# Four-layer graph block on one core: scores of the first four samples computed apart, wv fetched last, weights fetched through three queues, TensorE fed with ones at the start

## The chip, the cores and the metric

One core of a Trainium2 chip. The metric is the device time of one execution in microseconds (us). Five engines work side by side, each through its own instructions in order: TensorE (PE; its weight loads are listed as PEld), VectorE (DVE), ScalarE (ACT), GpSimd (POOL) and SyncE (SP), which only issues transfers here. Work that depends on another engine waits on a semaphore.

## The reference, cut to what matters

Four layers, each `x = layernorm(x + f(x, adj))`, on 128 samples of 128 nodes with 512 features, all in float32. The change touches layer 0 alone:

```
Xw = X @ Wv + bv
sj = Xw @ aw[:d, 0];  si = Xw @ aw[d:, 0]
e = leaky_relu(sj[:, None, :] + si[:, :, None] + ab[0], 0.2)
transition = row-normalised(A * exp(e))
H = 0;  Xk = X
for k in range(3):                # Wk has shape (3, 512, 512)
    H = H + Xk @ Wk[k] + bk[k]
    Xk = transition @ Xk
x = layernorm(x + relu(H))
```

The kernel computes `H` as `Y0 + T (Y1 + T Y2)` with `Yk = X @ Wk[k]`, and the scores `si`, `sj` as `X @ (Wv @ aw)`, so that Wv enters only through two columns of 512 numbers.

## The kernel before

**Products by seven.** Layer 0 takes four samples at a time (two pairs; 32 such groups). The product of four samples with a weight matrix is done by Strassen's scheme (Winograd's form) on two levels: `twice` (line 846) goes through seven combinations of the samples (`lefts`, line 809, made by GpSimd) and of the weights, called B11, B21, T2, T1, B22, T3 and N4 in the order of their use, and for each `strassen` makes seven products, each with a 128x128 block on the left and a row of weights on the right. That is 49 products a group. The right side is 386 columns wide (`QW`): 128 for each of the three Wk, and two that give the scores. Each product is two MATMUL records in the trace (and two LDWEIGHTS). The seven weight combinations lie in seven tiles "first" (`w7`), and each holds its own seven combinations again.

**Making the weights.** `prepare0` (line 898) does it. Wv (1 MB) is fetched by SP in two halves, wk by ACT and SP: columns 0 to 255 of each matrix as "low" and "high" rows (12 transfers of 64 KB each, together 1.5 MB), then columns 256 to 511 (12 of 128 KB, 1.5 MB, on SP). VectorE forms Wv @ aw by eight dot products ("junk" rows) against aw, which TensorE has spread over the partitions; ScalarE copies the two columns into the weight tiles B11 and B21, beside the copies of wk. `combine` (line 514) then makes the inner combinations of B11, B21 and B22 on VectorE, with ScalarE holding operands in PSUM, `combine_apart` (line 509) those of B12 on GpSimd, and `combine_once_more` (line 520) the outer ones: T1 and T2 on VectorE in seven steps, then T3 and N4 on GpSimd in four long subtractions.

**After the 49 products.** The results of a sample pair are collected in an "out" tile (`R`), to which VectorE and ScalarE add or copy each bank of PSUM. There are three such tiles and a group needs two. From the score columns of `R`, which are complete when B11 and B21 are through, the transition matrix is made: two transposes on TensorE, ScalarE's Prelu and Exp, a multiplication with adj and the row sums on VectorE, a scaling on GpSimd, a trip through DRAM ("e") and a 32x32 transposition. Only then can the "t" products (`T` times the collected columns, 512 wide) run, and after the last of them the `R` tile is free for the next group but one.

**What sets the order.** The program first writes all operations down with a key (a wished place, about one unit per sample pair) and then `Plan.order` (line 239) plays the whole kernel through with estimated durations: each engine takes, of the operations that could begin next, the one with the smallest key (or the earliest due time in later rounds, except on TensorE, which always goes by key). What comes out is a fixed order for each engine. SP may fetch a thing that depends on nothing only when TensorE has reached its key in the play:

```
285            for k, t in ready[e].items():
286                if e == SP and ops[k][8] > reached and not ops[k][4]:
287                    continue
288                t = max(t, free[e], port[e] if ops[k][6] else 0)
289                if e == SP:
290                    t = max(t, *(landed[j - LANES] - ISSUE * j for j in range(len(ops[k][1]))))
```

Keys that matter: x of group 0 has -9.5, of group 1 -1.0, of group 2 1.0; the products of group 0 run from 0 in steps of .28 (T1 has .84), its scores have .8, its "t" products 2.0; group 1 has two more on each.

Of the kernel before, what the change touches and what calls it, by code (L numbers as in the profile page):

```python
# [14 lines left out]
OP = mybir.AluOpType  # L15
AX = mybir.AxisListType

P = 128
# [8 lines left out]
U = 2  # L27
# [15 lines left out]
WHENV, WHENS, WHENP, WHENO = (.9, 1.9), (2.2, 3.2), (3, 4), (3.5, 4.5)  # L43
LAG1, LAG2 = 1, 1.5
COMBINE = (-9, -2), (-.5, -.2), .1
SOFT = .2
PARKED, LATE = .95, 4
RAMP = 0, 0, .05, 4
# [75 lines left out]
def estimate(engine, name, out, args, kw):  # L124

    n = out.idx.size if isinstance(out, View) else 0
    views = [a for a in args if isinstance(a, View)]
    psum = any(a.tile.kind in PSUM for a in views)
    scalars = sum(isinstance(a, View) and a.idx.size == 1 for k, a in [*enumerate(args), *kw.items()] if k != "accum_out")
    if engine == PE:  # L130
        return 107 if name == "transpose" else (1.74 if n <= P else 1.68) * n
    if name == "dma_start":
        return ISSUE
    if engine == DVE:
        if name == "bn_aggr":
# [12 lines left out]
    return 60 if name == "memset" else (740 - 160 * scalars if scalars else 180 + 3.2 * n) if n > 8 else 215  # L148


def shares_port(engine, name, args, kw):

    if engine == POOL:
        return name != "memset"
    views = [a for a in args if isinstance(a, View)]
    sbuf = [a for a in views[1:] if a.tile.kind not in PSUM and a.idx.size > 1]
    if engine != DVE or not sbuf:
        return False
    if name in ("tensor_scalar", "tensor_copy"):
        return "accum_out" not in kw and views[0].idx.size > 1  # L160
    return len(sbuf) > 1
# [12 lines left out]
class Plan:  # L174
# [64 lines left out]
    def order(self, urgent=None):  # L239
# [41 lines left out]
        def look(e):  # L281

            can = []
            soonest = math.inf
            for k, t in ready[e].items():
                if e == SP and ops[k][8] > reached and not ops[k][4]:
                    continue
                t = max(t, free[e], port[e] if ops[k][6] else 0)
                if e == SP:
                    t = max(t, *(landed[j - LANES] - ISSUE * j for j in range(len(ops[k][1]))))  # L290
                new = {}
                for tile in ops[k][5]:
# [21 lines left out]
        while count < n:  # L314
# [15 lines left out]
            free[e] = end = t + o[2]  # L330
            if o[7]:
                end = pipe = max(pipe, t + BEGIN) + o[7]
                landed += [end + LANDED] * len(o[1])
                landed = landed[-LANES:]
            if e == PE and o[8] > reached:
                reached = o[8]
                stale.add(SP)
# [52 lines left out]
def kernel(  # L390
# [73 lines left out]
    def four():  # L464

        return tile_of("four", U, D)
# [35 lines left out]

    def held_in_bank(kind, block):

        p = tile_of(kind, QW)
        ac.copy(p, block)
        return p

# [11 lines left out]
    def combine_once_more(W):  # L520

        base = plan.key
        for n, i in enumerate((B11, T1, T2, B21, T3, B22, N4)):
            plan.key = base + .1 * n
            c12, c22 = (held_in_bank(k, W[j][:, i, 0]) for k, j in (("t0", B12), ("t1", B22)))
            for to, a, b in ((T1, c12, B11), (T2, c22, T1)):
                ve.tensor_tensor(W[to][:, i, 0], a, W[b][:, i, 0], OP.subtract)
        flat = [w.rearrange("p j o f -> p (j o f)") for w in W]
        for to, a, b in ((T3, T2, B11), (N4, B21, T2)):
            for at in (slice(0, 4 * QW), slice(4 * QW, 7 * QW)):  # L530
                po.tensor_tensor(flat[to][:, at], flat[a][:, at], flat[b][:, at], OP.subtract)

    def prep():

# [363 lines left out]
    def prepare0():  # L898
        h = D // 2
        plan.key = -9.7  # L900
        awr = four().rearrange("p u f -> p (u f)")
        sp.dma_start(awr[:1], aw.rearrange("f o -> o f"), run=2 * D, parts=1)
        W = WT["0"] = [tile_of("w7", 7, 1, QW, place=(B11, B21, T2, T1, B22, T3, N4).index(k)) for k in range(7)]
        stage = [W[T2 + m].rearrange("p j o f -> p (j o f)")[:, :C * D].rearrange("p (c f) -> p c f", f=D)
                 for m in range(3)]

        def fetch(queue, dst, src, chunks, columns, run):
            with plan.together():
# [6 lines left out]
            at = chunks, slice(half * h, half * h + h)  # L915
            fetch(queue, stage[m][:, at[0], at[1]], wk0[m], *at, h)

        low, high, every = slice(0, 2), slice(2, 4), slice(0, 4)
        st = [four() for _ in range(2)]
        for g, chunks in enumerate((low, high)):  # L920
            plan.key = -9.7 + .2 * g
            fetch(sp, st[g], wv0, chunks, slice(0, D), D)
        plan.key = -9
        for m in range(3):
            fetch_part(ac, m, low, 0)
        awc, bvc = fixed(2 * C, name="aw_c"), fixed(C, name="bv_c")
        ab_b, bk0b = fixed(1, name="ab_b"), row()
        with plan.together():
            for c, v, n in ((awc, aw, 2 * C), (bvc, bv0, C)):
                ac.dma_start(c, bass.AP(tensor=v.tensor, offset=v.offset, ap=[[1, P], [P, n]]), run=1)  # L930
            ac.dma_start(bk0b[:3], bk0, parts=3)
            ac.dma_start(ab_b, rows(ab, 1), run=1)
        for m in range(3):
            fetch_part(sp if m else ac, m, high, 0)
        ones = fixed(P, name="ones")
        po.memset(ones, 1.0)
        awb = [bank() for _ in range(2)]
        for k in range(2):
            pe.matmul(awb[k], ones[:1], awr[:1, k * D:(k + 1) * D], start=True, stop=True)
        two = fixed(C, 2, name="cols0")  # L940
        for c in range(C):
            for k in range(2):
                dot(two[:, c, k:k + 1], st[c // 2][:, c % 2], awb[k])
        plan.key = WHEN0[0] + .05
        for m in range(3):
            fetch_part(sp, m, every, 1)
        plan.key = -9
        for g, half, j in ((0, 0, B11), (1, 0, B21), (0, 1, B12), (1, 1, B22)):
            for m in range(3):
                ac.copy(W[j][:, :4, :, m * P:(m + 1) * P].rearrange("p (n c) o i -> p c n (o i)", n=2),  # L950
                        stage[m].rearrange("p c (n i) -> p c n i", i=P)[:, 2 * g:2 * g + 2, 2 * half:2 * half + 2])
            scores = W[j][:, :4, 0, 3 * P:]
            if half:
                po.memset(scores, 0.0)
            else:
                po.memset(scores[:, 2:], 0.0)
                ac.copy(scores[:, :2], two[:, 2 * g:2 * g + 2])
            plan.key = COMBINE[half][g]
            (combine_apart if j in (B12,) else combine)(W[j])
            plan.key = -9  # L960
        plan.key = COMBINE[2]
        combine_once_more(W)
        plan.key = -9
        p = bank()
        aws = fixed(C, name="aw_sum")
        ve.tensor_add(aws, awc[:, :C], awc[:, C:])
# [3 lines left out]
                          start=j == 0, stop=j == C - 1)  # L970
        ve.tensor_tensor(c0, p[:, :1], ab_b, OP.add)

        p = bank()
        pe.matmul(p, ones[:3], bk0b[:3], start=True, stop=True)
        p = p.rearrange("p (h n i) -> p h n i", h=2, n=2)
        ac.copy(bias[:, 0], p[:, 0])
        ve.tensor_tensor(bias[:, 1], p[:, 1], bias[:, 0], OP.subtract)
        plan.key = WHENT[0][0] - .1
        for kind in ("t0", "t1"):
            p = tile_of(kind, D)  # L980
            pe.matmul(p, ones[:3], bk0b[:3], start=True, stop=True)
# [8 lines left out]
    def layer0(i0):  # L990
# [16 lines left out]
        def fresh(bs):  # L1007
            def takes(d):
# [7 lines left out]
                                         "p5": put(d22, bs[:, 1]), "c21": put(d21, bs[:, 0])}  # L1016
            return takes

        twice(left, WT["0"], QW, lambda r, half: [R[r][:, b, 2 * half + n] for b in range(U) for n in range(2)],
              lambda r, half: [R[r][:, b, 2 * half:2 * half + 2] for b in range(U)],  # L1020
              [fresh(bias[:, half]) for half in range(2)], .28)
        yield
        loads = []
        for r, i in enumerate(both):
            A = load_adj(i)
            plan.key = base + WHENT[0][r]
            s = col(U)
            ac.activation(s, R[r][:, :, 0, 3 * P + 1], AF.Identity, bias=c0)
            pt = spread_pair([R[r][:, b, 0, 3 * P:3 * P + 1].to_broadcast([P, P]) for b in range(U)])
# [570 lines left out]
```

## Time and profile before

| | |
|---|---|
| time before, median of 3 runs | 5380.56 us (5377.26 to 5382.14) |
| the profiled execution's own time | 5377.98 us |
| its span in the trace | 5376.2 us |
| PE, share of the span | 99% (5307.6 us) |
| DVE, POOL, ACT | 82%, 73%, 45% |
| mean granted clock of TensorE | 0.998 |

A time outside the span (1.8 us) is what lies before the first and after the last instruction. Nearly all lines of the page are named L381, the line from which the planner emits; so an instruction is told by what it writes and reads: "bank<-first,four" is a product of layer 0 (weights "first", samples "four"), "first" as target is work on the weights, "out" the collecting of results, "junk" the dot products with Wv. A timeline line has the start, the time from the first start to the last end of the merged instructions, the engine, the operation and its count, and in brackets the idle time before and who ended it. The windows view has for each stretch its length, and per engine the busy time and the number of instructions; then the granted clock, the share of the DMA engines and GB/s.

### The profile page before, as it was taken

To read this page: it belongs to the slowest core of one execution; us is meant where nothing else is said; L and a number is where in the kernel's file an instruction comes from. 1 tells how busy PE (TensorE), PEld (TensorE's weight loads), DVE (VectorE), ACT (ScalarE), POOL (GpSimd) and SP (SyncE) were. 2 spreads that over 40 slices of the span, in tenths; PEclk is the share of its full clock that TensorE was granted. 3 is DMA by queue.
4 is the path that set the end of the run, shared out by engine and by line. 5 is a ranking of instruction groups with operands and counts; after the bars stand their busy time and mean duration, and the time that the engine had idled before them with its cause. 6 is when DMAs were issued, how large, how long until landed. Compare 5 with 4: busy or idle time off the path is not lost.

```text
span 5376.2 us, 92973 instructions
## 1 busy us (share of the span) xinstructions
PE 5307.6 (99%) x29039; PEld 4230.2 (79%) x29039; DVE 4423.1 (82%) x11721; ACT 2407.2 (45%) x6085; POOL 3906.2 (73%) x4937
## 2 busy tenths in 40 slices
PE   8999999999999999999999999999999999999998
PEld 4555555555888888888888889988998899889987
DVE  7788887887888888888888778887877888888876
ACT  3343343344544444444444344444444444444444
POOL 6777787676766666666666577777877777777776
PEclk9999999999999999999999999999999999999999
DMA  4544544445544454444444745555555455555543
GB/s 108 142 136 131 148 135 139 121 115 190 167 143 147 157 163 144 147 159 161 143 148 152 233 140 163 160 159 151 164 161 158 154 163 158 161 152 162 161 146 111
DMA packets 831143, 813.61 MB, mean 151 GB/s; under 512 B 258348, under 2 KB 631604, under 8 KB 830648
## 3 DMA queue, kind: packets, MB, share of 16 engines
q1 hardware_dynamic: 827650, 806.60, 48.9%
q8 instruction: 231, 3.78, 0.3%
q14 instruction: 264, 2.16, 0.1%
q10 hardware_dynamic: 2998, 1.06, 0.1%
HBM read 458.38 MB, written 349.04 MB: 150 GB/s over the span
## 4 chain that ended last, share of the span: by engine, by line
PE 88%; DVE 7%; issue 2%; DMA 1%; ACT 1%; POOL 1%; SPq 0%; ACTq 0%; DVEq 0%; POOLq 0%
PE bank L381 67%; PE t L381 21%; DVE four L381 2%; DVE out L381 1%; DVE col L381 1%; DVE first L381 1%; DVE junk L381 1%; POOL out L381 0%; ACT out L381 0%; DVE side L381 0%; ACT four L381 0%; DVE rows L381 0%; DVE bank L381 0%; DMA first<-in_L_gnn_Wk_dram 0%; SPq L381 0%
## 5 line engine op out<-in xcount | busy, mean ns | idle before, releaser
L381 PE MATMUL bank<-first,four 128*128 128x386 f32 (+3 forms) x6352 | 1748.6, 423 | 23.6 <-ACT first L381 9.9
L381 PEld LDWEIGHTS bank<-first,four 128*128 128x128 f32 (+2 forms) x6352 | 1089.3, 187 | 600.2 <-DVE out L381 101.9
L381 DVE TENSOR_TENSOR out<-bank,out 128x386 f32<-128x386 f32 (+1 forms) x1942 | 948.5, 507 | 253.1 <-PE bank L381 194.8
L381 DVE TENSOR_TENSOR four<-bank,four 128x256 f32<-128x256 f32 x1113 | 453.9, 416 | 151.3 <-PE bank L381 138.9
L381 POOL TENSOR_TENSOR out<-out 128x772 f32<-128x772 f32 (+3 forms) x249 | 341.6, 1381 | 272.9 <-DVE out L381 215.4
L381 POOL TENSOR_TENSOR four<-four 128x256 f32<-128x256 f32 (+2 forms) x434 | 351.5, 823 | 189.1 <-DVE four L381 140.6
L381 PE MATMUL bank<-first,out 128*128 128x256 f32 (+1 forms) x1746 | 432.4, 377 | 3.7 <-DVE four L381 1.6
L381 POOL TENSOR_TENSOR four<-four,four 128x256 f32<-128x256 f32 (+2 forms) x467 | 397.0, 855 | 10.0 <-PE bank L381 1.5
L381 POOL TENSOR_TENSOR col<-col,neghalf 128x2 f32<-128x2 f32 x320 | 227.9, 712 | 231.7 <-DVE col L381 230.5
L381 ACT COPY out<-bank 128x258 f32<-128x258 f32 (+2 forms) x489 | 194.9, 404 | 440.7 <-PE bank L381 359.9
L381 PEld LDWEIGHTS bank<-first,out 128*128 128x128 f32 (+1 forms) x1746 | 318.5, 188 | 65.4 <-issue 9.0
L381 ACT ACTIVATE four<-four,col,col 128x512 f32<-128x512 f32 (+1 forms) x355 | 308.5, 892 | 125.4 <-POOL col L381 118.9
L381 DVE TENSOR_TENSOR first<-bank,first 128x256 f32<-128x256 f32 (+1 forms) x591 | 240.4, 415 | 97.9 <-PE bank L381 89.3
L381 PE MATMUL bank<-first 128*128 128x128 f32 (+1 forms) x2132 | 297.6, 278 | 1.6 <-DVE four L381 1.6
L381 DVE BATCH_NORM_STATS2 col<-four 128x6 f32<-128x512 f32 x424 | 282.9, 681 | 10.5 <-ACT four L381 9.1
L381 ACT COPY four<-bank 128x256 f32<-128x256 f32 (+1 forms) x358 | 150.6, 424 | 303.8 <-PE bank L381 287.7
L381 PEld LDWEIGHTS bank<-first 128*128 128x128 f32 (+1 forms) x2132 | 270.0, 190 | 15.9 <-issue 4.0
L381 PE MATMUL t<-out,sq 128*128 128x512 f32 x512 | 256.3, 593 | 0.5 <-ACT t L381 0.5
L381 ACT COPY t<-out 128x512 f32<-128x512 f32 x256 | 150.9, 591 | 235.4 <-PE bank L381 73.7
L381 PE MATMUL t<-first,four 128*128 128x256 f32 (+2 forms) x1064 | 250.3, 361 | 0.6 <-DVE four L381 0.6
L381 PE MATMUL bank<-out,first 128*128 128x128 f32 (+3 forms) x1432 | 232.4, 312 | 2.2 <-DVE col L381 1.8
L381 PE MATMUL bank<-four,first 128*128 128x128 f32 (+3 forms) x1400 | 220.5, 303 | 2.4 <-DVE four L381 1.3
(526 smaller groups left out, 13149.7 us busy)
## 6 DMA issues: line engine op xcount, KB each, us to landing
h<-four SPq DMA_DIRECT2D x69, 512.0 KB, 3.3
four<-in_x_dram SPq DMA_DIRECT2D x256, 128.0 KB, 3.4
four<-h SPq DMA_DIRECT2D x64, 512.0 KB, 4.6
four<-in_x_dram SPq DMA_DIRECT2D x62, 512.0 KB, 4.5
x1d<-four SPq DMA_DIRECT2D x62, 512.0 KB, 2.9
four<-x1d SPq DMA_DIRECT2D x60, 512.0 KB, 4.5
out<-h SPq DMA_DIRECT2D x55, 512.0 KB, 5.1
h<-out SPq DMA_DIRECT2D x50, 512.0 KB, 3.2
```

The costliest lines, as they stand in the source:

```text
L381: call(*map(real, args), **{n: real(a) for n, a in kw.items()})
```

## The change

Six edits, all in layer 0's preparation and first group, and in the planner's costs.

1. **Order of fetches.** aw, Wv and the small vectors are no longer fetched first. bk goes first on SP, then x. The low rows of wk's first half go through ACT's queue, the high rows through POOL's (12 transfers of 64 KB each), the second half on SP. Wv, aw, bv and ab follow on SP with key .8.
2. **The first group without score columns.** In group 0 the seven weight combinations are used 384 columns wide. Their dot products come at key .8; then 16 products of a 128x128 block of x with the two columns (`two`) give the scores straight into `R`, at key .9.
3. **`score_columns`.** The score columns of the seven weight combinations, which groups 1 to 31 need, are made directly from the two columns by some thirty small copies, subtractions and fills on ScalarE and GpSimd.
4. **The combinations on GpSimd** leave out the two columns (128x1536 and 128x1152 instead of 1544 and 1158), with the same count.
5. **32 products of 128x128 ones**, into a bank that nobody reads, with key -9.9: TensorE's first work.
6. **Planner.** A transfer on POOL costs it 1000 ns, doesn't share VectorE's port, and doesn't count for the eight lanes of outstanding transfers; those on ACT now do.

```diff
+SCORE0 = .8
+WARM = 32
...
     if name == "dma_start":
-        return ISSUE
+        return 1000 if engine == POOL else ISSUE
...
     if engine == POOL:
-        return name != "memset"
+        return name not in ("memset", "dma_start")
...
-                if e == SP:
+                if ops[k][7] and e != POOL:
...
         for to, a, b in ((T3, T2, B11), (N4, B21, T2)):
-            for at in (slice(0, 4 * QW), slice(4 * QW, 7 * QW)):
-                po.tensor_tensor(flat[to][:, at], flat[a][:, at], flat[b][:, at], OP.subtract)
+            for at in (slice(0, 4), slice(4, 7)):
+                po.tensor_tensor(W[to][:, at, 0], W[a][:, at, 0], W[b][:, at, 0], OP.subtract)
+
+    def score_columns(W, two):
+        last = lambda j: W[j][:, :, 0, 3 * P:]
+        sc = fixed(3, 7, 2, name="cols7")
+        po.memset(sc, 0.0)
+        for j in (B22, T3):
+            po.memset(last(j), 0.0)
+        for k in range(2):
+            top, low = two[:, 2 * k], two[:, 2 * k + 1]
+            ac.copy(sc[:, k, B11], top)
+            ac.copy(sc[:, k, T2], top)
+            ac.copy(sc[:, k, B21], low)
+            po.tensor_tensor(sc[:, k, T1], sc[:, k, T3], top, OP.subtract)
+            po.tensor_tensor(sc[:, k, N4], low, top, OP.subtract)
+        po.tensor_tensor(sc[:, 2], sc[:, 1], sc[:, 0], OP.subtract)
+        for j, k in ((B11, 0), (B21, 1), (T2, 0), (N4, 2)):
+            ac.copy(last(j), sc[:, k])
+        po.tensor_tensor(last(T1), last(T3), sc[:, 0], OP.subtract)
...
+        for g, chunks in enumerate((slice(0, 2), slice(2, 4))):
+            plan.key = -9
+            for m in range(3):
+                fetch_part((ac, po)[g], m, chunks, 0)
+        plan.key = WHEN0[0] + .05
+        for m in range(3):
+            fetch_part(sp, m, slice(0, 4), 1)
...
+        plan.key = -9.9
+        warm = bank()
+        with plan.together(1.25):
+            for _ in range(WARM):
+                pe.matmul(warm[:, :P], ones, ones, start=True, stop=True)
...
+        plan.key = SCORE0
+        awr = prep()
+        sp.dma_start(awr[:1], aw.rearrange("f o -> o f"), run=2 * D, parts=1)
+        st = [prep().rearrange("p (u f) -> p u f", f=D) for _ in range(2)]
+        for g in range(2):
+            fetch(sp, st[g], wv0, slice(2 * g, 2 * g + 2), slice(0, D), D)
...
+        two = WT["cols"] = fixed(C, 2, name="cols0")
+        for c in range(C):
+            for k in range(2):
+                dot(two[:, c, k:k + 1], st[c // 2][:, c % 2], awb[k])
...
-        plan.key = WHENT[0][0] - .1
+        plan.key = SCORE0
         for kind in ("t0", "t1"):
...
+        wide = QW if i0 else 3 * P
...
+        if not i0:
+            two = WT["cols"]
+            plan.key = base + SCORE0 + .1
+            pt = bank()
+            with plan.together(30):
+                for r in range(2):
+                    for b in range(U):
+                        at = 2 * (U * r + b)
+                        for c in range(C):
+                            pe.matmul(pt[:, at:at + 2], xT[r][:, b, c], two[:, c], start=r == b == c == 0,
+                                      stop=c == C - 1, skip_group_check=True)
+            for r in range(2):
+                ac.copy(R[r][:, :, 0, 3 * P:], pt[:, 2 * U * r:2 * U * r + 2 * U].rearrange("p (b k) -> p b k", k=2))
+            score_columns(WT["0"], two)
+            plan.key = base
...
-            plan.key = base + WHENT[0][r]
+            plan.key = base + (WHENT[0][r] if i else max(WHENT[0][r], SCORE0 + .2))
```

More of the change, by code (lines that the diff above doesn't have):

```diff
@@ L332, in order @@
                 end = pipe = max(pipe, t + BEGIN) + o[7]
-                landed += [end + LANDED] * len(o[1])
-                landed = landed[-LANES:]
+                if e != POOL:
+                    landed += [end + LANDED] * len(o[1])
+                    landed = landed[-LANES:]
             if e == PE and o[8] > reached:
@@ L503, in held_in_bank @@
     def held_in_bank(kind, block):
-        p = tile_of(kind, QW)
+        p = tile_of(kind, 3 * P)
         ac.copy(p, block)
@@ L527, in combine_once_more @@
                 ve.tensor_tensor(W[to][:, i, 0], a, W[b][:, i, 0], OP.subtract)
-        flat = [w.rearrange("p j o f -> p (j o f)") for w in W]
         for to, a, b in ((T3, T2, B11), (N4, B21, T2)):
-            for at in (slice(0, 4 * QW), slice(4 * QW, 7 * QW)):
-                po.tensor_tensor(flat[to][:, at], flat[a][:, at], flat[b][:, at], OP.subtract)
+            for at in (slice(0, 4), slice(4, 7)):
[17 more added lines that the diff above has]
+        po.tensor_tensor(last(T1), last(T3), sc[:, 0], OP.subtract)
     def prep():
@@ L900, in prepare0 @@
         plan.key = -9.7
-        awr = four().rearrange("p u f -> p (u f)")
-        sp.dma_start(awr[:1], aw.rearrange("f o -> o f"), run=2 * D, parts=1)
+        bk0b = row()
+        sp.dma_start(bk0b[:3], bk0, parts=3)
         W = WT["0"] = [tile_of("w7", 7, 1, QW, place=(B11, B21, T2, T1, B22, T3, N4).index(k)) for k in range(7)]
@@ L905, in prepare0 @@
                  for m in range(3)]
+        W = [w[:, :, :, :3 * P] for w in W]
         def fetch(queue, dst, src, chunks, columns, run):
@@ L916, in fetch_part @@
             fetch(queue, stage[m][:, at[0], at[1]], wk0[m], *at, h)
[L918 to L922, printed above, removed]
-        plan.key = -9
[L924 to L934, printed above, removed]
+        for g, chunks in enumerate((slice(0, 2), slice(2, 4))):
[5 more added lines that the diff above has]
+            fetch_part(sp, m, slice(0, 4), 1)
+        plan.key = -9
         ones = fixed(P, name="ones")
         po.memset(ones, 1.0)
[L937 to L946, printed above, removed]
-        plan.key = -9
+        plan.key = -9.9
[3 more added lines that the diff above has]
+                pe.matmul(warm[:, :P], ones, ones, start=True, stop=True)
+        plan.key = -9
+        p = bank()
+        pe.matmul(p, ones[:3], bk0b[:3], start=True, stop=True)
+        p = p.rearrange("p (h n i) -> p h n i", h=2, n=2)
+        ac.copy(bias[:, 0], p[:, 0])
+        ve.tensor_tensor(bias[:, 1], p[:, 1], bias[:, 0], OP.subtract)
         for g, half, j in ((0, 0, B11), (1, 0, B21), (0, 1, B12), (1, 1, B22)):
@@ L951, in prepare0 @@
                         stage[m].rearrange("p c (n i) -> p c n i", i=P)[:, 2 * g:2 * g + 2, 2 * half:2 * half + 2])
[L952 to L957, printed above, removed]
             plan.key = COMBINE[half][g]
@@ L962, in prepare0 @@
         combine_once_more(W)
-        plan.key = -9
+        plan.key = SCORE0
[4 more added lines that the diff above has]
+            fetch(sp, st[g], wv0, slice(2 * g, 2 * g + 2), slice(0, D), D)
+        awc, bvc = fixed(2 * C, name="aw_c"), fixed(C, name="bv_c")
+        ab_b = fixed(1, name="ab_b")
+        with plan.together():
+            for c, v, n in ((awc, aw, 2 * C), (bvc, bv0, C)):
+                sp.dma_start(c, bass.AP(tensor=v.tensor, offset=v.offset, ap=[[1, P], [P, n]]), run=1)
+            sp.dma_start(ab_b, rows(ab, 1), run=1)
+        awb = [bank() for _ in range(2)]
+        for k in range(2):
+            pe.matmul(awb[k], ones[:1], awr[:1, k * D:(k + 1) * D], start=True, stop=True)
+        two = WT["cols"] = fixed(C, 2, name="cols0")
+        for c in range(C):
+            for k in range(2):
+                dot(two[:, c, k:k + 1], st[c // 2][:, c % 2], awb[k])
         p = bank()
@@ L971, in prepare0 @@
         ve.tensor_tensor(c0, p[:, :1], ab_b, OP.add)
[L973 to L977, printed above, removed]
-        plan.key = WHENT[0][0] - .1
+        plan.key = SCORE0
         for kind in ("t0", "t1"):
@@ L1017, in fresh @@
             return takes
-        twice(left, WT["0"], QW, lambda r, half: [R[r][:, b, 2 * half + n] for b in range(U) for n in range(2)],
-              lambda r, half: [R[r][:, b, 2 * half:2 * half + 2] for b in range(U)],
+        wide = QW if i0 else 3 * P
+        twice(left, [w[:, :, :, :wide] for w in WT["0"]], wide,
+              lambda r, half: [R[r][:, b, 2 * half + n, :wide] for b in range(U) for n in range(2)],
+              lambda r, half: [R[r][:, b, 2 * half:2 * half + 2, :wide] for b in range(U)],
               [fresh(bias[:, half]) for half in range(2)], .28)
+        if not i0:
[13 more added lines that the diff above has]
+            plan.key = base
         yield
```

## The prediction

> **What bounds the kernel now.** I read the page first (PE 99%), then the stretches, then TensorE's timeline of the first 70 us, and then, for each gap in it, the engine that ended it.
>
> The stretches (window, length, PE busy, PEld, DVE, ACT, POOL, clock, DMA share, GB/s):
>
> ```profile
> 0.00:20.00 20.00, 7.66 (x15) 3.55 (x15) 4.76 (x13) 5.62 (x10) 3.87 (x17) 1.00 0.73 174
> 20.00:40.00 20.00, 15.41 (x34) 7.11 (x34) 18.44 (x40) 11.02 (x26) 13.36 (x16) 1.00 1.02 181
> 40.00:60.00 20.00, 18.02 (x41) 7.81 (x40) 12.95 (x32) 7.00 (x18) 18.36 (x17) 0.83 0.14 33
> 60.00:80.00 20.00, 19.68 (x60) 10.98 (x60) 17.16 (x39) 7.20 (x16) 19.69 (x22) 1.00 0.14 40
> 160.00:200.00 40.00, 40.00 (x133) 22.73 (x132) 32.23 (x84) 17.65 (x42) 28.22 (x32) 1.00 0.46 128
> ```
>
> Behind 60 us TensorE is never short of work; what the change can move lies in the first 60. There busy time misleads, so I count products. In dense work (1240.01 to 1249.09, 28 records) a 386-wide record takes .324 us, a product .65; a 512-wide record .43. TensorE's timeline:
>
> ```profile
> 19.88 2.94 PE L381 MATMUL bank<-first,four 128*128 128x386 f32 x4 [9.95 <-ACT first L381]
> 24.75 10.34 PE L381 MATMUL bank<-first,four 128*128 128x386 f32 x24 [1.93 <-DVE out L381]
> 35.37 1.56 PE L381 MATMUL bank<-first,four 128*128 128x386 f32 x4 [0.29 <-DVE out L381]
> 39.30 0.92 PE L381 MATMUL bank<-first,four 128*128 128x386 f32 x2 [2.37 <-DVE first L381]
> 41.41 1.07 PE L381 MATMUL bank<-first,four 128*128 128x386 f32 x2 [1.19 <-issue]
> 42.85 2.82 PE L381 MATMUL bank<-first,four 128*128 128x386 f32 x4 [0.38 <-DVE first L381]
> ...
> 60.37 7.40 PE L381 MATMUL bank<-first,four 128*128 128x386 f32 x22 [0.32 <-DVE out L381]
> 67.61 1.88 PE L381 MATMUL t<-out,sq 128*128 128x512 f32 x4
> ```
>
> By 60.37 us it has done 68 records (34 products), four 512-wide ones and two transposes: 68 x .324 + 1.7 + .2 = 24.0 us of dense work. So 36.4 us are lost: 19.9 before the first product; 17.05 - 10.4 = 6.7 up to 36.93; 5.9 - 1.3 = 4.6 up to 42.85; 17.5 - 10.4 - 1.9 = 5.2 after. The 36.4 are the whole stake, .7% of the time.
>
> What held it? ScalarE's timeline:
>
> ```profile
> 13.79 0.62 ACT L381 COPY first<-first 128x512 f32<-128x512 f32 x1 [1.79 <-DMA first<-in_L_gnn_Wk_dram]
> ...
> 19.63 0.20 ACT L381 COPY first<-cols 128x4 f32<-128x4 f32 x1 [2.84 <-DVE junk L381]
> ...
> 25.24 0.20 ACT L381 COPY first<-cols 128x4 f32<-128x4 f32 x1 [2.01 <-DVE junk L381]
> ```
>
> The weights of B11 are there at 14.4 and wait until 19.6 for their score columns, hence for Wv, its dot products and the VectorE queue; B21 waits the same way until 25.2. From 36.9 to 42.9 the gap is ended by "DVE first": VectorE is busy for all of 28 to 46 with the T1 and T2 weights and the collecting of B11's and B21's results.
>
> **The change part by part**, against the profiled execution (5378.0 us, 2.6 below the median).
>
> *Start.* Four small transfers leave ACT's queue (0.72 to 2.87), so low wk lands 2.1 us earlier: the copy at 13.79 comes at 11.7, the first product at 12.5. The second needs a sum from GpSimd, which first has 12 transfers to issue. No row shows GpSimd issuing one; SP's take .45 to .54 us each, and one GpSimd subtraction of 128x512 takes 1.27. Between 12 x .5 = 6 and 12 x 1.3 = 15 us I take 12, as the other engines' issues would have to double for it: GpSimd is free at 14, and products stream from 16 instead of 24.75. B11 and B21 (14 products, 9.1 us) end near 25.5 instead of 35.1. That alone is no gain: T2 waits for the second half of wk.
>
> *Second half.* It lands at 26.15 (chain of waits). Ahead of it lay 1 MB of Wv; at the 209 GB/s of 18 to 36 us that is 5.0 us, so 21.2. From landing to the 21st product (T2's last, 46.6) it took 20.4 us, and in that time VectorE spent about 7.5 us on B11's and B21's evictions, combinations and a transposition, which are then behind it. Between nothing and all of it saved I take 4: T2 ends at 37.6, **9 us earlier** (5 to 12.5).
>
> *Clock.* Records follow one another at .64 us between 20.7 and 21.3, half rate, and after the gap the granted clock falls to .5 for 42.0 to 45.4 and again for 52.2 to 55.6; the second costs 1.7 us behind T2. With shorter gaps I take **2** (0 to 3.4). The 32 products of ones end at half rate at 1 + 32 x 2 x .21 = 15 us, at full rate at 8; they bring the first 12 products at most 3.9 us, which the wait for the second half swallows. The Trainium skill, "TensorE: Matmul & The Clock Gate", section "Why this matters for your kernels", speaks against this edit: a pause of more than about 3 us returns the clock to half, so the ones must run up to the stream itself. The trace agrees on the size (idle from 36.9 to 39.3 and 39.8 to 41.4, half clock at 42.0). Where a wait in the new order reaches that length, the rule gives one more 3.4 us window at half rate, 1.7 us, and the sum 9.3 instead of 11.0; by the rows, with gaps cut short, it stays.
>
> *Filling.* While T2's weights are made, TensorE may take group 1's B11, whose x stands behind wk on SP as before: 7 x .65 = **4.5** (0 to 4.5). Not more, as its B21 needs the "out" tile that group 0 still holds.
>
> *Added.* Wv must be reached by TensorE's key .8, about when T1 begins (29), and takes 1 MB / 209 GB/s + 2 to 3 us: landed near 37. Then on TensorE: 16 score products, 32 records at .116 (half of bv_c's 1.86 / 8, which ran at half rate) = 3.7; aw spread, 4 x .43 = 1.7; aw_sum .9: together 6.3, free where TensorE waits anyway. I take **-4** (-6.3 to -2). Eight dot products at .78 = 6.2 us go from VectorE's idle time to its busiest, so the scores stand at 45 to 50. The small operations of `score_columns` (ACT .2, POOL .1 to .45 each) lie beside that, and group 1 needs them only for B11's last columns; if group 1's B11 waits for them, the filling is gone, which its bound covers.
>
> *Late scores.* The chain from transposes to the first "t" product took 45.51 to 67.61, 22.1 us, 3 of them behind GpSimd's 3.2 us subtraction:
>
> ```profile
> 47.77 6.33 POOL L381 TENSOR_TENSOR first<-first 128x1544 f32<-128x1544 f32 x2 [1.62 <-DVE first L381]
> 54.09 1.19 POOL L381 TENSOR_SCALAR sq<-sq,col 128x128 f32<-128x128 f32 x2
> ```
>
> So "t" comes at 67 to 72. By then TensorE can have done at most 49 products of group 0 and B11 and T1 of group 1: 63 x .65 = 40.9, + 1.9. With 25.4 us lost it runs dry at 68. I take **-.5**.
>
> Sum: 9 + 2 + 4.5 - 4 - .5 = **11.0 us**, 5367.0 for the profiled kind of run, 5369.5 at the median: 5369. The other queue edits: the Trainium skill, "DMA: Bandwidth & Descriptors", section "Issuing engines are not separate DMA queues", says that all queues end on the same 16 engines and a further one saves only issue time. The trace has the DMA share at .77 between 8 and 18 us and 1.14 between 18 and 36. By the rule POOL's queue helps the first stretch alone, and the sum would stand, as I credit it with nothing.
>
> **The rivals.**
> - *A, as summed*, 5358 to 5369.8: 47%. For it: the gap lines name score columns and VectorE.
> - *B, the scores become the wait.* "t" at 72 to 79: each us past 68 costs one, so 3 to 11 lost of 11; 5373 to 5380. For: 6.2 us of dots meet a VectorE busy 100%. Against: T1 and B11 of group 1 fill. 25%.
> - *C, slower.* Same place, one mechanism: both "out" tiles of group 0 are held until "t", the third is filled by group 1's B11 and T1, and TensorE stands. No gain is left when "t" comes at 36.4 + 42.8 = 79; slower by over 0.2% (10.8 us) from 90 on. It takes Wv landing 20 us later than I have it, which happens if its fetch stands in SP's queue behind an x load that waits for a buffer, as SP did for 6.4 us (DVE four) and 12 us (POOL sq) in the first 70 us. At 95 it gives 5396. 17%.
> - *D, the edits don't do what they say.* GpSimd's issues take 2 us each: sums from 25, B21's weights late, T2 only 3 us earlier without filling: 3 + 2 - 4 = 1; 5379. 11%.
>
> **How the numbers follow.** 0.2%, about what a measurement of this kernel can tell from no change, is 10.8 us. Faster by more: A, .47. Within: B and D, .36. Slower: C, .17. The range takes A, B and D and leaves out C: low 5358 (12.5 + 3.4 + 4.5 - 2 = 18.4 gained, and 4 more for the order of the rest), high 5383 (D with its -6.3).
>
> **What would show it.** The first 384-wide product near 12.5 and a stream from 16; no "PE <- ACT first" of 9.9 us; the second half of wk landed near 21; T2's 21st product near 38; clock 1.00 between 40 and 56; first "t" product before 72. Wrong if GpSimd's first sum comes after 20, if VectorE's junk rows stand between T1/T2 rows, or if TensorE has a gap of over 3 us just ahead of the first "t".

## The result

The changed kernel is **slower**: 5389.94 us (5384.41 to 5395.76) against 5379.3 us (5374.16 to 5384.02), medians of 20 runs each, ratio 1.0020 [1.0014, 1.0026], or 10.6 us. Its profiled span is 5387.1 us, against 5376.2. All lines now bear the name L384.

TensorE's timeline of the changed kernel (start, time, what; in brackets the idle time before and who ended it):

```profile
1.13 9.90 PE L384 MATMUL bank<-ones 128*128 128x128 f32 x64 [1.13 <-POOL ones L384]
...
15.25 7.10 PE L384 MATMUL bank<-first,four 128*128 128x384 f32 x12 [3.18 <-ACT first L384]
...
40.20 1.12 PE L384 MATMUL t<-row,ones 3*128 3x512 f32 x2
41.25 0.91 PE L384 MATMUL bank<-first,four 128*128 128x384 f32 x2
42.09 1.12 PE L384 MATMUL t<-row,ones 3*128 3x512 f32 x2
43.05 1.04 PE L384 MATMUL bank<-ks,ones 1*128 1x512 f32 x2
44.02 1.65 PE L384 MATMUL bank<-first,four 128*128 128x384 f32 x2
48.87 1.65 PE L384 MATMUL bank<-first,four 128*128 128x384 f32 x2 [3.20 <-DVE out L384]
50.32 1.71 PE L384 MATMUL bank<-bv_c,aw_sum 128*128 128x1 f32 x8
51.88 2.91 PE L384 MATMUL bank<-first,four 128*128 128x384 f32 x4
54.58 6.83 PE L384 MATMUL bank<-cols,four 128*128 128x2 f32 x32
61.27 1.63 PE L384 MATMUL bank<-first,four 128*128 128x384 f32 x2
62.69 0.64 PE L384 MATMUL bank<-ident,out 128*128 128x128 f32 x2
63.12 15.65 PE L384 MATMUL bank<-first,four 128*128 128x384 f32 x46
78.61 1.02 PE L384 MATMUL t<-out,sq 128*128 128x512 f32 x2
```

The stream begins at 15.25 instead of 24.75, as the change means it to. But from 54.58 the 16 score products take 6.83 us, and 128x384 records around them .73 to .82 us each (2.91 / 4, 1.63 / 2) where 46 of them later take .34. Two stretches of the same kernel (length; busy time and count of PE, PEld, DVE, ACT, POOL; granted clock; DMA share; GB/s):

```profile
43.50:54.00 10.50, 7.30 (x18) 4.12 (x17) 8.08 (x19) 1.53 (x9) 8.70 (x8) 0.52 0.19 50
54.00:64.00 10.00, 10.00 (x40) 8.68 (x39) 0.96 (x3) 1.59 (x7) 4.95 (x4) 0.50 0.00 0
```

TensorE is busy in all of 54 to 64 and yet at half clock. In before these stretches have .83 and .92. In after the granted clock fell to half at 43.9 and came back to full at 64.4.

For all comparisons I count **lost time** at a moment as the prediction does: the time minus the dense cost of the records done by then (.324 us for a 384- or 386-wide one, .429 for a 512-wide, .109 for a transposition; the ones, the score products and the products that spread and sum aw count as no work). "At 80" and "80 to 1000" are in us:

| | at 43 | at 80 | 80 to 1000 |
|---|---|---|---|
| before | 30.2 | 35.6 | 17.1 |
| after | 24.9 | 42.0 | 21.8 |

So the start does win 5.3 us; then, up to 80 us, after loses 11.7 more than before and stands 6.4 behind. Up to 1000 us it loses another 4.7, in work that the change does not touch, and the spans end 10.9 apart.

### The profile page after: what moved, and what is told of

It is laid out like the page before. It is cut to its first block, busy times and chain, and to the rows that moved or that the text cites. A ratio compares the mean times of both kernels' runs of the same rounds, so it can differ in the third digit from the quotient of the medians.

```text
span 5387.1 us, 93181 instructions
## 1 busy us (share of the span) xinstructions
PE 5323.4 (99%) x29135; PEld 4249.1 (79%) x29135; DVE 4424.7 (82%) x11721; ACT 2409.1 (45%) x6095; POOL 3910.8 (73%) x4954
## 4 chain that ended last, share of the span: by engine, by line
PE 88%; DVE 7%; issue 2%; DMA 1%; ACT 1%; POOL 1%; SPq 0%; ACTq 0%; DVEq 0%; POOLq 0%
PE bank L384 67%; PE t L384 21%; DVE four L384 2%; DVE out L384 1%; DVE col L384 1%; DVE junk L384 1%; DVE first L384 1%; DMA four<-in_x_dram 0%; ACT out L384 0%; POOL out L384 0%; ACT four L384 0%; DMA first<-in_L_gnn_Wk_dram 0%; DVE side L384 0%; POOL four L384 0%; DVE bank L384 0%
## 5 line engine op out<-in xcount | busy, mean ns | idle before, releaser
L384 PE MATMUL bank<-first,four 128*128 128x386 f32 (+4 forms) x6352 | 1752.9, 423 | 16.3 <-DVE out L384 6.8
L384 PEld LDWEIGHTS bank<-first,four 128*128 128x128 f32 (+2 forms) x6352 | 1091.0, 187 | 593.0 <-DVE out L384 111.2
L384 DVE TENSOR_TENSOR out<-bank,out 128x386 f32<-128x386 f32 (+2 forms) x1942 | 949.7, 507 | 260.8 <-PE bank L384 206.1
L384 DVE TENSOR_TENSOR four<-bank,four 128x256 f32<-128x256 f32 x1113 | 454.5, 416 | 151.2 <-PE bank L384 139.5
L384 POOL TENSOR_TENSOR out<-out 128x772 f32<-128x772 f32 (+4 forms) x249 | 340.9, 1378 | 272.6 <-DVE out L384 211.6
L384 POOL TENSOR_TENSOR four<-four 128x256 f32<-128x256 f32 (+2 forms) x434 | 349.9, 819 | 168.3 <-DVE four L384 114.1
L384 PE MATMUL bank<-first,out 128*128 128x256 f32 (+1 forms) x1746 | 432.5, 378 | 3.5 <-DVE four L384 1.6
L384 POOL TENSOR_TENSOR four<-four,four 128x256 f32<-128x256 f32 (+2 forms) x467 | 396.3, 853 | 10.5 <-PE bank L384 2.6
L384 ACT COPY out<-bank 128x258 f32<-128x258 f32 (+3 forms) x491 | 195.1, 402 | 454.9 <-PE bank L384 361.8
L384 POOL TENSOR_TENSOR col<-col,neghalf 128x2 f32<-128x2 f32 x320 | 227.9, 712 | 233.3 <-DVE col L384 231.7
L384 PEld LDWEIGHTS bank<-first,out 128*128 128x128 f32 (+1 forms) x1746 | 319.0, 189 | 64.7 <-issue 9.0
L384 ACT ACTIVATE four<-four,col,col 128x512 f32<-128x512 f32 (+1 forms) x355 | 308.1, 892 | 123.4 <-POOL col L384 122.1
L384 DVE TENSOR_TENSOR first<-bank,first 128x256 f32<-128x256 f32 (+1 forms) x591 | 240.7, 416 | 98.2 <-PE bank L384 87.2
L384 PE MATMUL bank<-first 128*128 128x128 f32 (+1 forms) x2132 | 297.6, 278 | 1.6 <-DVE four L384 1.6
L384 DVE BATCH_NORM_STATS2 col<-four 128x6 f32<-128x512 f32 x424 | 283.2, 682 | 10.5 <-ACT four L384 9.1
L384 ACT COPY four<-bank 128x256 f32<-128x256 f32 (+1 forms) x358 | 150.7, 424 | 302.4 <-PE bank L384 281.3
L384 PEld LDWEIGHTS bank<-first 128*128 128x128 f32 (+1 forms) x2132 | 269.9, 190 | 15.7 <-issue 3.8
L384 PE MATMUL t<-out,sq 128*128 128x512 f32 x512 | 256.6, 594 | 2.6 <-ACT t L384 1.7
L384 ACT COPY t<-out 128x512 f32<-128x512 f32 x256 | 150.8, 591 | 232.4 <-PE bank L384 102.6
L384 PE MATMUL t<-first,four 128*128 128x256 f32 (+2 forms) x1064 | 249.8, 360 | 0.6 <-DVE four L384 0.6
L384 PE MATMUL bank<-out,first 128*128 128x128 f32 (+3 forms) x1432 | 232.6, 312 | 2.2 <-DVE col L384 1.8
L384 POOL TENSOR_SCALAR sq<-sq,col 128x128 f32<-128x128 f32 x256 | 153.4, 607 | 96.8 <-DVE col L384 93.9
```

The lines of the kernel that those rows point to most:

```text
L384: call(*map(real, args), **{n: real(a) for n, a in kw.items()})
```

## The experiments

Two questions: what takes the 11.7 us (the score products at half clock, the dot products on VectorE, late scores that hold the tiles), and what the 4.7 are. Times are medians beside runs of the kernel before on the same chip (5376.4 to 5377.9).

**One score product.** After, with one eight-column product for the 16, and the planner's duration set so that the order of all else stays. It leaves out 15 of the 16.

```diff
-            with plan.together(30):
+            with plan.together(120):
-                for r in range(2): ... pe.matmul(pt[:, at:at + 2], xT[r][:, b, c], two[:, c], ...)
+                pe.matmul(pt[:, :4 * U], xT[0][:, 0, 0], two.rearrange("p c k -> p (c k)"), start=True, stop=True)
```

> The changed kernel with one product of eight columns in place of the 16 score products of group 0, at the same planned cost, so that the order of everything else stays; it leaves out 15 of the 16 products, so group 0's scores are not the reference's. Theory S (the scores' way through TensorE is what costs): the 16 took 6.8 us at half clock, so the time falls by 6 to 10 us against the changed kernel, to 5380 to 5384, and the first t product comes at 70 to 72 instead of 78.6. Theory O (what costs is the different order of the rest of the kernel): within 3 us of the changed kernel, as the lost time is made up before 100 us anyway. Theory Q (the ones or GpSimd's queue cost): no change beyond 2 us.

5379.99, ratio 1.0005 [.9996, 1.0014]. The excess over before falls from 10.6 to 2.1 us, which is theory S in the time (6 to 10 us less); the first "t" product comes at 73.30, a little later than it said. 36.6 are lost at 80. TensorE's timeline of it:

```profile
55.67 0.43 PE L384 MATMUL bank<-cols,four 128*128 128x8 f32 x2
55.95 1.63 PE L384 MATMUL bank<-first,four 128*128 128x384 f32 x2
...
57.80 15.66 PE L384 MATMUL bank<-first,four 128*128 128x384 f32 x46
```

6.83 - .43 = 6.4 us of the row go, and full clock is back at 59.1 instead of 64.4.

**Wide scores.** If narrow records keep the clock down, the same 32 with 64 times the columns should cost no more time. Each two columns are repeated 64 times; the order stays.

```diff
-                            pe.matmul(pt[:, at:at + 2], xT[r][:, b, c], two[:, c], ...)
+                            pe.matmul(pt[:, at:at + P].rearrange("p (m k) -> p m k", k=2), xT[r][:, b, c],
+                                      two[:, c][:, None, :].to_broadcast([P, P // 2, 2]), ...)
```

> The changed kernel with each of the 16 score products 128 columns wide instead of two (the two columns repeated 64 times), at the same planned cost and so in the same order; the result is the same. Theory H (the narrow products leave TensorE's array nearly idle and so keep the clock at half): with the array in use the clock returns to full within some 4 us, and although each product streams 64 times as many columns the 16 take 5 to 7 us as before and what follows runs at full clock from 58 us instead of 64; 2 to 4 us faster than the changed kernel, ratio to before 1.0013 to 1.0016. Theory L (the narrow products cost their weight loads alone, the clock would have come back no later without them): 16 products at half clock take 7 us or more, and the time is that of the changed kernel or up to 2 us longer.

5384.25, 1.0012 [1.0003, 1.0020]; 38.8 lost at 80. TensorE's timeline of it:

```profile
55.51 4.28 PE L384 MATMUL bank<-cols,four 128*128 128x128 f32 x32
59.63 0.81 PE L384 MATMUL bank<-first,four 128*128 128x384 f32 x2
...
60.49 15.14 PE L384 MATMUL bank<-first,four 128*128 128x384 f32 x46
```

The 64-fold width takes 2.55 us less than the narrow row, as theory H foresaw. The clock is back at 56.6, inside the row, where after has it at 64.4. At one and the same clock the width costs nothing: at half clock a record starts .21 us behind the one before it in either row, at full clock .11 (here behind 56.6; for two columns in the next run). The phase of the clock's steps is not the same in the two runs, so the clock's return would be weak evidence alone.

**Wv fetched between.** Wv goes ahead in the play, so that the scores might come earlier.

```diff
-        plan.key = SCORE0
+        plan.key = -5
         awr = prep()
 ...
             sp.dma_start(ab_b, rows(ab, 1), run=1)
+        plan.key = SCORE0
         awb =
```

> The changed kernel with the fetch of aw, Wv and the small vectors at key -5, between the two halves of wk, all else as it is. Theory S: the dot products move out of VectorE's full stretch, the scores are ready by 35 us, TensorE has no hole at 44 to 54; 5370 to 5382, while the second half of wk lands 5 us later. Theory O: 5387 to 5393, since the order of the rest is still another one than before. Theory Q: as the changed kernel, 5388 to 5392.

5388.54, 1.0020 [1.0011, 1.0029]; 40.2 lost at 80. A miss, of theory S at least, and the time is that of theories O and Q: SP still issued Wv behind wk, at 21.0 instead of 26.66, and the score products, by their key, did not move (55.15). But it shows the clock by itself. TensorE's timeline, then two-microsecond stretches around that row:

```profile
49.91 5.41 PE L384 MATMUL bank<-first,four 128*128 128x384 f32 x16
55.15 3.87 PE L384 MATMUL bank<-cols,four 128*128 128x2 f32 x32
58.88 1.63 PE L384 MATMUL bank<-first,four 128*128 128x384 f32 x2
```

```profile
54.00:56.00 2.00, 2.00 (x14) 1.47 (x12) 1.75 (x4) 0.00 (x0) 0.59 (x1) 1.00 0.00 0
56.00:58.00 2.00, 2.00 (x20) 2.00 (x20) 0.00 (x0) 0.00 (x0) 2.00 (x3) 1.00 0.68 193
58.00:60.00 2.00, 2.00 (x9) 1.59 (x10) 0.00 (x0) 0.68 (x4) 1.12 (x1) 0.60 0.31 69
```

Here the narrow row starts at full clock, TensorE has no idle time, and 3.2 us into the row, at 58.4, the clock **falls** to half. By the timeline the 3.4 us before that are the narrow row but for the first .2.

**Short dots**, **short both**, **short dots with a reduction.** The dot products over 8 columns instead of 512 (the rest of them is left out), alone; with one score product; and with `aw_sum` formed otherwise. The order stays.

```diff
-                dot(two[:, c, k:k + 1], st[c // 2][:, c % 2], awb[k])
+                with plan.together(7.97):
+                    dot(two[:, c, k:k + 1], st[c // 2][:, c % 2, :8], awb[k][:, :8], 8)
 ... the third one also:
-        ve.tensor_add(aws, awc[:, :C], awc[:, C:])
+        ve.tensor_reduce(aws, awc.rearrange("p (k c) -> p c k", k=2), AX.X, OP.add)
```

> The changed kernel with the eight dot products of Wv with aw over 8 columns instead of 512, at the same planned cost, so the order stays; it leaves out the rest of each dot product, so the scores are not the reference's. Each falls from .77 us to about .25, 4.2 us of VectorE in all. Theory S with the dots as a cause (they hold up the collecting of results from 44 to 49 us): the hole before the product at 48.9 closes and the time falls by 4 to 7 us, to 5383 to 5386. Theory N (the narrow products alone matter): within 2 us of the changed kernel, 5388 to 5392.

> The changed kernel with the short dot products and one score product of eight columns in place of 16, order and planned costs as in the changed kernel; it leaves out most of the score computation of Wv and of group 0. Theory S: what is left is the start alone, which was 5 us ahead of before at 43 us, and the time falls below before, to 5372 to 5377. Theory N: as with one score product alone, 5379 to 5381. Theory O (the order of the rest costs 4 us or more by itself): 5378 or more.

> The kernel with the short dot products (the rest of each left out) and the sum of aw's halves made by a reduction over one operand instead of an addition of two, at the same planned cost and in the same order. In the run with short dot products this addition of four columns took 4.04 us, from 46.5 until GpSimd's subtraction ended at 50.4. Theory P (VectorE is held because both its operands lie in SBUF while GpSimd works): the reduction takes under .3 us, the products behind it move up by 3 to 4 us, and the time is 3 to 5 us under that run, ratio to before 1.0012 to 1.0016. Otherwise it takes as long as the addition and the ratio stays at 1.0021.

5388.62, 1.0021 [1.0012, 1.0029], 43.1 at 80; 5380.0, 1.0008 [.9999, 1.0017], 34.4; 5385.61, 1.0014 [1.0006, 1.0023], 39.9 (short dots, short both and short dots with a reduction, in this order). The first gained nothing, for a reason that I had not foreseen. VectorE, then GpSimd, in short dots:

```profile
46.46 4.04 DVE L384 TENSOR_TENSOR aw_sum<-aw_c 128x4 f32<-128x4 f32 x1
```

```profile
44.96 2.93 POOL L384 TENSOR_TENSOR first<-first 128x1536 f32<-128x1536 f32 x1
47.82 0.49 POOL L384 TENSOR_TENSOR four<-four,four 128x128 f32<-128x128 f32 x1
48.23 2.25 POOL L384 TENSOR_TENSOR first<-first 128x1152 f32<-128x1152 f32 x1
```

An addition of four columns lasts 4.04 us and ends with GpSimd's run of subtractions, 50.5. In after the same one took .31, in wide scores 1.78 and in short both 3.71, and there too it ended with a subtraction of GpSimd (51.0 and 50.1). The Trainium skill, "GPSIMD Engine Reference", section "Specifications", says that GpSimd shares its SBUF interfaces with VectorE and contends with instructions that have two SBUF inputs; it gives no size. As a reduction with one operand, under the same subtractions:

```profile
45.54 0.14 DVE L384 TENSOR_REDUCE aw_sum<-aw_c 128x4 f32<-128x8 f32 x1
```

This is theory P, in the time too (1.0012 to 1.0016 foreseen). So the dot products cost 2.1 us at 80 (42.0 - 39.9). From one score product to short both it is 36.6 - 34.4 = 2.2, but short both has the held addition, for which TensorE waits 1.99 us, so there the dot products by themselves may cost more. Short both did not fall below before, as theory S wanted; it fits theories N and O.

**The other edits alone.** Before, with the 32 products of ones; before, with the high rows of wk through POOL and the planner's edits for it; after, with one of the 32 ones and the same order. The first two have a new order of instructions too.

```diff
 ones alone:       +            for _ in range(32): pe.matmul(warm[:, :P], ones, ones, start=True, stop=True)
 POOL queue alone: -            fetch_part(sp if m else ac, m, high, 0)
                   +            fetch_part(po, m, high, 0)
 one of the ones:  -WARM = 32
                   +WARM = 1
```

> The kernel before with the 32 products of ones as TensorE's first work, nothing else changed. Theory S: within 3 us of before (5376 to 5382), since the first products wait for scores until 19.9 whatever the clock, and the ones end at 11. Theory Q: 3 us or more slower, as aw's spread and with it the dot products come later. Theory O: anything within 6 us of before, by the new order alone.

> The kernel before with the high rows of wk's first half fetched through GpSimd's queue and the planner's costs for that, nothing else changed. Theory S: within 4 us of before (5375 to 5383), rather faster, as Wv's second half no longer stands behind eight wk transfers on SP. Theory Q: slower by 3 us or more, with the first sums of x late on GpSimd. Theory O: anything within 6 us of before.

> The changed kernel with one product of ones in place of 32, at the same planned cost, so the order stays. Theory S: within 2 us of the changed kernel (5388 to 5392), since in its trace the clock is at half again from 12.7 to 19.5, which is where the first 12 real records lie, and then returns by itself. If the ones do keep TensorE fast for the first products: 2 to 4 us slower, 5392 to 5394. If they delay them: faster by 1 us or more.

5376.18, .9999 [.9990, 1.0008]; 5375.36, .9996 [.9987, 1.0005]; 5384.41, 1.0014 [1.0006, 1.0023] (ones alone, POOL queue alone, one of the ones). The ones bring nothing that can be measured, in either kernel: with one of them the excess over before is 8.0 us instead of 10.6, a little more than the 2 us that theory S allowed, and the intervals overlap. The queue leaves 31.4 lost at 80, 4.2 fewer than before, and gives 2.0 of them back by 1000 us. In its trace the clock, once full at 29.9, does not fall again in the first stretch, where before has 6.8 us at half; half of that, an estimated 3.4, would be most of the 4.2. Why it stays up was not tested.

**Order alone.** Before, with one of the planner's constants moved by 1%, which changes nothing but the order of instructions; later by 1.5%, for three kernels: after, the queue alone, and "scores earlier". This last is after with Wv's key as above, wide score products at key .5, the reduction, and group 0's transition at the keys of before; it was run with both constants.

```diff
-ISSUE, BEGIN, LANES, LANDED = 450, 1000, 8, 2050
+ISSUE, BEGIN, LANES, LANDED = 450, 1010, 8, 2050
```

> The kernel before with one of the planner's constants moved by 1% (BEGIN, the planned delay of a transfer, 1010 instead of 1000 ns): no operation changes, only the order, and that nearly everywhere. Theory O (a new order alone is worth some us either way): 5 us or more away from before, in either direction. Theory S: within 4 us of before, 5374 to 5382.

> The changed kernel with four edits: Wv's fetch not held back by TensorE's key, the score products 128 columns wide at key .5 instead of .9 with a planned cost of .22 us each, the sum of aw's halves by a reduction, and group 0's transition at the keys of before; the result is the same. If the scores' place and price are the cause (theory S), the first t product comes before 70 us and the time is at or under that of before, ratio .999 to 1.0005. If the order of the rest decides (theory O), 1.001 or more whatever the start does.

> The changed kernel with the planner's BEGIN at 1015 instead of 1000 ns: the same operations in another order nearly everywhere. Theory O (the loss between 80 and 1000 us comes with any order that is not before's): some 19 to 22 us lost in that stretch against before's 17.1, and a ratio to before of 1.001 to 1.003. Theory C (it belongs to the change's own order): a stretch loss that differs by 3 us or more from the changed kernel's 21.8. The score products still run at key .9, so up to 80 us it stays behind before by 4 us or more under both.

> The kernel with the score products wide and earlier, with BEGIN at 1015 ns, so in another order. Theory O: 2 us or more ahead of before at 80 us, and 2 to 6 us given back by 1000 us, ratio .9995 to 1.001. Theory C: the lead at 80 us stays to the end, ratio at or under .9995.

> The kernel before with GpSimd's queue alone, with BEGIN at 1015 ns. It led before by 4 us at 80 us and kept 2 of them at the end. Theory O: a lead at 80 us of 1 to 5 us, and 1 to 4 us given back by 1000 us, ratio .999 to 1.0008. Theory C: the whole lead is kept, ratio .9985 to .9993.

| | time | ratio | at 80 | 80 to 1000 |
|---|---|---|---|---|
| before, 1010 | 5380.98 | 1.0008 [.9999, 1.0017] | 34.7 | 20.3 |
| scores earlier | 5380.5 | 1.0005 [.9996, 1.0014] | 32.7 | 22.9 |
| after, 1015 | 5380.9 | 1.0008 [.9999, 1.0017] | 42.3 | 20.0 |
| scores earlier, 1015 | 5372.19 | .9991 [.9982, 1.0000] | 33.1 | 20.3 |
| POOL queue alone, 1015 | 5369.14 | **.9986 [.9977, .9995]** | 30.8 | 19.0 |

After loses as much in the first 80 us under both orders; its excess over before is 10.6 us with the first and 3.1 with the second. Most of the gain lies between 3000 and 4000 us, in later layers. In these 1000 us TensorE is busy for 987.79 in after and for 992.48 with 1015; for the queue alone it is 988.02 and 992.76, for scores earlier 987.93 and 991.97, and for before 988.38.

The forecasts of these runs came out mixed. Scores earlier has its first "t" product at 69.04 and the ratio 1.0005, the upper end of theory S. Before with 1010 moved by 4.5 us, between its two theories. After with 1015 lost 20.0 us between 80 and 1000, as theory O said. Scores earlier with 1015 and the queue alone with 1015 gave part of their lead back by 1000 us, which is theory O, and yet ended at ratios of theory C, since neither theory had the gain behind 3000 us.

TensorE's timeline of scores earlier shows what the mended change does at its own place:

```profile
25.54 9.21 PE L384 MATMUL bank<-first,four 128*128 128x384 f32 x20 [8.13 <-DVE out L384]
34.59 3.73 PE L384 MATMUL bank<-cols,four 128*128 128x128 f32 x32
...
49.47 19.73 PE L384 MATMUL bank<-first,four 128*128 128x384 f32 x60
69.04 1.02 PE L384 MATMUL t<-out,sq 128*128 128x512 f32 x2
```

9.3 us fewer are lost at 80 than in after, 2.9 fewer than in before, and the stretch up to 1000 us takes 5.8 back (22.9 against 17.1). POOL queue alone with 1015 beats both kernels, by some 8.6 us against before. Some of that is the queue's (4.8 us ahead at 80), some the order's; POOL queue alone with the old constant shows that the first without the second can't be told from no change. Before itself was not run with 1015, so how much of the 8.6 us that constant would bring without the queue stays open.

## Why the prediction was wrong

The forecast was 11 us faster; measured were 10.6 slower, outside the range.

- **Start: right, in part by luck.** "Products stream from 16": 15.25. Two errors cancelled. GpSimd's issues cost less than I took, .55 us each for the first nine instead of 1.0; the last ended at 8.80 and the first sum began at 9.62, not 14. But the low rows of wk did not land 2.1 us earlier: the copy that waits for them ahead of the first product, at 13.79 in before, came at 14.58 and not at 11.7, and the first product at 15.25 instead of 12.5.
- **Second half: right.** Its copy came at 21.29 (21.2 forecast for the landing) and T2's 21st product ended at 38.9, 7.7 us earlier than in before (9 forecast). Up to 43 us 5.3 us are won in lost time.
- **"Added", the first step that failed.** I priced 32 records at .116, full clock, 3.7 us. The price is right for full clock (.11 in the run with Wv between), but they ran at half: .213 each, 6.83. Cut to one product, the kernel's excess falls by 8.5 us. The mistake was to price an operation by a clock that I assumed and to set the clock in another step as if the two were independent.
- **"Clock", the second.** Forecast was 1.00 between 40 and 56. Measured: half from 43.9 to 64.4, 20.5 us, where before has 6.8 in this stretch (42.0 to 45.4, 52.2 to 55.6). The mechanism was wrong as well: I laid the falls to gaps and hoped for shorter ones. The clock's steps lie 3.4 us or multiples of it apart in these traces, so I look at the 3.4 us ahead of a fall. In after TensorE has no idle time in those before 43.9; about 2.6 of them are the products with three rows or one (40.20 to 44.02 in the timeline of the result). Before had shown it already. Ahead of 42.0 its two pauses last 2.37 and 1.19 us (the second begins at 40.2, not at 39.8), so neither reaches the 3 us that I read into them; and ahead of the fall at 52.2 its TensorE goes on without a pause:

```profile
48.66 1.12 PE L381 MATMUL t<-row,ones 3*128 3x512 f32 x2
49.71 0.92 PE L381 MATMUL bank<-first,four 128*128 128x386 f32 x2
50.55 1.12 PE L381 MATMUL t<-row,ones 3*128 3x512 f32 x2
```

In after a gap of 3.20 us before 48.87 lies in the half clock too, and behind that come only narrow records and few wide ones. In the run with Wv fetched between, the narrow row alone brought the clock down. That products with three rows or one do the same is what the two falls suggest; no run takes them out. (The windows view gives 1.00 for the first 20 us of before, although records there come .64 us apart at 20.7, which is half rate: where the trace has no entry for the clock, up to 28.3 us there, the view prints 1.00.)
- **"Filling", the third.** Nothing filled. Group 1's x was transposed on VectorE only at 46.94 and 49.44, the first behind all eight dot products, the second also behind three results and aw_sum, as this view of after's VectorE shows, and its first 386-wide product came at 80.97:

```profile
46.32 0.69 DVE L384 SCALAR_TENSOR_TENSOR junk<-rows,bank 128x512 f32<-128x512 f32 x1
...
46.94 1.24 DVE L384 STREAM_TRANSPOSE four<-four 128x1024 f32<-128x1024 f32 x1
...
49.44 1.23 DVE L384 STREAM_TRANSPOSE four<-four 128x1024 f32<-128x1024 f32 x1
```

- **"Late scores": later than forecast, and no wait.** "t" came at 78.61 and not at 67 to 72, yet TensorE has no gap before it: group 0's own products, held up by 43 to 63, still fill 63.12 to 78.6. So neither rival B nor C happened, though C had the sign. What C foresaw, TensorE standing because of "t", is seen nowhere; the loss lies 20 us earlier, where I had put a gain. One sign of being wrong did come: dot products stand among VectorE's T1 and T2 rows (38.07, between 36.86 and 38.68).
- **What I left out: the order of the rest.** I gave it 4 us at one end of the range; after lost 4.7 more than before between 80 and 1000 us. Before's 17.1 is the least of 16 traces (18.4 to 22.9 in the others; 19.2 to 21.8 in those with after's order). The order of before was a lucky one there, as far as one trace tells, and any change of order was likely to lose 1 to 6 us. With the order held, the traces still differ by 2.6, so a part of the 4.7 may be chance. I could not have told that from one trace, but the range should have held it.

The sum: the score products cost 5.4 us at 80 (42.0 - 36.6) and the dot products 2.1; without both 34.4 are lost, 1.2 fewer than in before. Of the 5.3 won at 43 the other 4.1 go to what remains of 43 to 60 us in short both: the spread of aw, aw_sum with TensorE's wait of 1.99 us for it, and half clock from 41.8 to 55.5, which I did not separate. So 5.4 + 2.1 - 1.2 + 4.7 = 11.0, against 10.9 between the two spans; the terms are differences between neighbouring runs, so that they add up proves little, and the 4.7 is the weakest of them. That products of two columns do not keep the clock up is shown; how narrow is too narrow was not measured. Why the order with 1015 gains in the later layers was not traced either.

On the ones: the Trainium skill, "TensorE: Matmul & The Clock Gate", section "Why this matters for your kernels", says that a pause of over about 3 us returns the clock to half. After the ones and the small products behind them TensorE stood 3.18 us and the clock was half from 13.2 to 20.0, but it fell 1.1 us into the pause, so after's trace does not show that rule at work. In the trace of one score product, where the pause lasts 5.22 us, the clock fell at 14.7, 3.5 us into it, which fits. The same page, section "What's actually happening", has half clock as the state behind an idle window. The run with Wv fetched between fell to half at 58.4 with PE busy all the time, so here the measurement decides: being busy with products of two columns did not keep the clock up.

## What to carry to other kernels

Price a tiny matmul by its weight load at the clock that it will really have (here 6.83 / 16 = .43 us for a product of two columns at half clock, 3.87 / 16 = .24 mostly at full), and do not count on it to raise the clock: put it amid wide work, or give it width, which here cost nothing at the same clock. When work moves to a busy engine, look at what then stands behind it there; here the x of the next group, which was to fill the gap. And in a kernel whose order is planned by a list, compare with versions that differ in the order alone, since here the medians of such versions lay 4 to 9 us apart, nearly as much as the change moved, though most of their intervals touch.

## What the runs showed of the hardware

- 32 records of 128x2 with a weight load each took 6.83 us at half clock; 64 times as wide 4.28, as the clock rose within them. At one clock both widths take the same, .21 us a record at half and .11 at full. TensorE at 100% busy and half clock stand side by side for 10 us.
- The clock fell with TensorE busy throughout: behind 3.2 us of products of two columns (58.4, Wv fetched between), and behind a stretch that is mostly products with three rows or one (43.9 in after).
- An addition of 128x4 on VectorE took 4.04 us while GpSimd subtracted (.15 to 3.71 in other runs of it); the reduction of the same data .14.
- GpSimd issued nine transfers of 64 KB in 5.00 us (.55 each), about what SP takes.
